# A state-space scan, attention and a mixture of experts on one core: two PSUM buffers for the first image's scan inputs, ranks by broadcasts, group norm sums on ScalarE

## The chip, the core and the metric

One core of a Trainium2 chip runs the whole program. The metric is the device time of one execution in microseconds (us). The engines' short names are those of the profile: PE (TensorE), DVE (VectorE), ACT (ScalarE), POOL (GpSimd), SP (SyncE, which issues nearly all DMAs here).

## What is computed

Four images of 384 channels by 32 x 32 positions go through two layers. Cut to what matters:

```python
# layer 0: group norm over 32 groups, then a selective scan in four directions
xs = _cross_scan(_gn(x))                      # rows, columns, both reversed: K = 4
x_dbl = einsum('bkdl,kcd->bkcl', xs, x_proj_weight)
dts, Bs, Cs = x_dbl[:, :, :12], x_dbl[:, :, 12:28], x_dbl[:, :, 28:]
dt = softplus(einsum('bkrl,kdr->bkdl', dts, dt_projs_weight) + dt_projs_bias)
# for each image, direction, channel d and state n (16 states), along 1024 positions:
h = h * exp(dt * A[d, n]) + (dt * u) * B[n]
y = sum over n of h * C[n]
y = _cross_merge(ys + Ds * u)
x = x + gelu(layernorm_over_channels(y))
# layer 1, on 1024 tokens of 384
t = t + causal_attention(_ln_t(t))            # one head of 384
z = _ln_t(t)
probs = softmax(z @ gate_w + gate_b)          # 4 experts
masked = probs of the two largest, others 0, divided by their sum + 1e-9
t = t + sum over e of masked[e] * (gelu(z @ w1[e] + b1[e]) @ w2[e] + b2[e])
```

Ties in the two largest go to the lower index. Everything is float32.

## The kernel before

**Units.** A scan instruction works on 128 partitions by 1024 positions: 32 channels by 4 states. An image has 192 such units (`IMAGE`: 3 chunks of 128 channels, 4 directions, 4 groups of states, 4 groups of 32 channels), four images have 768. For unit n, `decay` (L505) makes exp(dt*A) on ACT, `front` (L512) makes v = (dt*u) * B on DVE into PSUM (`ps_b`, one buffer of two banks), `middle` (L518) is the scan h on DVE, `back` (L525) multiplies h by C in place on POOL, and `row` (L550) sums over states on PE into another two banks, for four units at a time. The dt and dt*u of 32 channels, each repeated on four partitions, come by DMA from a scratch in DRAM (`spread_dt`, L473: tiles dt4 and du4, four buffers each); B and C come as one tile bc for four units by two DMAs (`spread_bc`, L484; two buffers). `fetch(t)` issues dt4 for unit t+5, du4 for t+3 and, where t+3 is a multiple of four, bc for t+3.

**Order.** The program is written out by hand. A loop over ticks t issues, in this order: `decay(t+2)`, what `due` holds for the tick, `front(t)`, `back(t-1)` with an added wait on `front(t)` ("beside a scan"), what `inner` holds, parked generators (`unpark`), `middle(t)`, `row(t-2)` on every fourth tick, `fetch(t)`, one step of the preparation of a later image, and then PE work. Each engine runs its own instructions in this order. PE work comes from generators that yield the time they expect to need; a tick grants 4.4 us of it in attention (`PACE_A`) and 3.3 in the experts (`PACE_E`). "wait" n puts a generator off by n ticks, "inner" parks it until the next tick's place between `back` and `middle`.

**Preparation.** `preparation(b)` does `groupnorm` (bn_stats L302, bn_aggr L303, then group means by small matmuls), `project_x` (rows of B and C, and the low-rank dt) and `project_dt` (softplus on ACT, the product dt*u on DVE, L395, and their stores to DRAM), for image b while the image before is scanned. `fold` (in `later`) multiplies the query and key weights in the first image.

**PE's banks.** Four PSUM banks (`banks`, class `Shared`) are taken and given back by name in first-in order; each taking makes a new tile. `project_dt` needs two at once.

**After an image's scans** `evict` (L570) and `finish` (layer norm, gelu, the sum with x, L707) leave the tokens yb. `behind(b)` then runs `attention(b)` and `experts(b)`, one image after the other. `attention` takes the buffer `a0` for its normalised tokens axn at its start; the same buffer holds `both` (named fx in the profile) of the experts of the image before, whose half `acc` is stored to `out` by `store` (L999), four ticks after the last expert. The subtraction of the mean into axn is L601, its last factor L649. `gates` finds each token's two best experts by comparing each expert with the others, one after the other (L901 to L915), with 16 elements in a partition.

The last image's attention and experts have nothing beside them: the scans end at 3237 us.

Of the kernel before, what the change touches and what calls it, by code (L numbers as in the profile page):

```python
# [15 lines left out]
P = 128  # L16
# [31 lines left out]
def hybrid_kernel(  # L48
# [53 lines left out]
    class Shared:  # L102
# [20 lines left out]
        def give(self, *names):  # L123
            for name in names:
                self.free.append((clock[0] + self.rest, self.taken.pop(name)))

    banks = Shared(
        BANKS, lambda i, name: ps_m.tile([P, 512], F32, tag=f"pm{i}", name=name), 0
    )
    slots = Shared(  # L130
        SLOTS, lambda i, name, *shape: slotp.tile(list(shape), F32, tag=f"s{i}", name=name), 1
# [68 lines left out]
    a4 = const.tile([P, K * NG, NQ], F32, tag="a4", name="a4")  # L200

    sel = const.tile([P, DJ], F32, tag="sel", name="sel")
    dump = const.tile([P, 1], F32, tag="dump", name="dump")
    nc.scalar.activation(a_raw, a_raw, AF.Exp)
    nc.scalar.activation(dump, eps, AF.Sqrt)
# [91 lines left out]
    def groupnorm(b, u):  # L297
        st = sm.tile([P, M, NH, 6], F32, tag="gn_st", name=f"gn_st_{b}")
        mv = sm.tile([P, M, 2], F32, tag="gn_mv", name=f"gn_mv_{b}")
        for m in range(M):  # L300
            for h in range(NH):
                nc.vector.bn_stats(st[:, m, h, :], u[m][:, h * 512 : (h + 1) * 512])  # L302
            nc.vector.bn_aggr(mv[:, m, :], st[:, m].rearrange("p h s -> p (h s)"))  # L303
            if b == 0 and m == 0:
                pgb = group_weights()
            yield "wait", 1
        if b == 0:
            nc.vector.tensor_scalar_mul(gback, pgb[:NGRP, :C], float(C // NGRP))
        mean_c = sm.tile([P, M], F32, tag="gn_mc", name=f"gn_mc_{b}")
        nc.vector.tensor_copy(mean_c, mv[:, :, 0])  # L310
        yield "wait", 1
        mean = sm.tile([P, M], F32, tag="gn_mean", name=f"gn_mean_{b}")
        ps = yield from over_group(mean_c, f"mean_{b}")
        nc.vector.tensor_copy(mean, ps)
        banks.give(f"gn_mean_{b}")
        dev = sm.tile([P, M], F32, tag="gn_dev", name=f"gn_dev_{b}")
        nc.vector.tensor_sub(dev, mean_c, mean)
        nc.vector.tensor_mul(dev, dev, dev)
        nc.vector.tensor_add(dev, dev, mv[:, :, 1])
        yield "wait", 1  # L320
        rstd = sm.tile([P, M], F32, tag="gn_rstd", name=f"gn_rstd_{b}")
        ps = yield from over_group(dev, f"var_{b}")
        nc.scalar.activation(rstd, ps, AF.Sqrt, bias=eps)
        banks.give(f"gn_var_{b}")
        yield "wait", 1
        nc.vector.reciprocal(rstd, rstd)
        nc.vector.scalar_tensor_tensor(mean, mean, -1.0, rstd, ALU.mult, ALU.mult)
        for m in range(M):
            if b == 0 and m == 1:
                nc.vector.tensor_scalar(  # L330
                    u[m], u[m], rstd[:, m : m + 1], mean[:, m : m + 1], ALU.mult, ALU.add
                )
            else:
                nc.scalar.activation(
                    u[m], u[m], AF.Identity, bias=mean[:, m : m + 1], scale=rstd[:, m : m + 1]
                )
            nc.sync.dma_start(xn_d[b][:, m, :], u[m])
            yield "wait", 1
# [169 lines left out]

    def front(n):
        u = units[n]  # L510
        u["v"] = ps_b.tile([P, L], F32, tag="v", name=f"v_{u['name']}")
        return nc.vector.tensor_tensor(u["v"], spread["du4", n], spread["bc", n][:, 0, :], ALU.mult)  # L512

    def middle(n):
# [62 lines left out]
            waiting.append(behind(b))  # L577


    def layernorm(dst, src, name, lag):  # L580

        width = dst.shape[2]
        n = width // 512
        mus = []
        for h in range(n):  # L590
            mu = yield from banks.take(f"mu_{name}_{h}")
            for c in range(M):
                nc.tensor.matmul(
                    mu, mean_w, src[:, c, bass.ts(h, 512)], start=(c == 0), stop=(c == M - 1)
                )
            mus.append(mu)
            yield "pe", 2.6
        yield "inner", 0
        for h in range(n):
            s = bass.ts(h, 512)  # L600
            nc.vector.tensor_tensor(  # L601
                dst[:, :, s], src[:, :, s], mus[h].unsqueeze(1).to_broadcast([P, M, 512]),
                ALU.subtract,
            )
            banks.give(f"mu_{name}_{h}")
        sqs = []
        for c in range(M):
            sq = yield from slots.take(f"sq_{name}_{c}", P, width)
            sqs.append(sq)
        for h in range(n):  # L610
            for c in range(M):
                s = bass.ts(h, 512)
                nc.scalar.activation(sqs[c][:, s], dst[:, c, s], AF.Square)
        yield "wait", lag
        var = yield from banks.take(f"var_{name}")
        for h in range(n):
            for c in range(M):
                for q in range(4):
                    o = h * 512 + q * P
                    nc.tensor.matmul(  # L620
                        var[32 * q : 32 * (q + 1), h * P : (h + 1) * P], mean_w[:, :32],
                        sqs[c][:, o : o + P], start=(c == 0), stop=(c == M - 1),
                        tile_position=(0, 32 * q),
                    )
            yield "pe", 1.0
        slots.give(*[f"sq_{name}_{c}" for c in range(M)])
        rs = one.tile([P, n, P], F32, tag=f"rs{n}", name=f"rs_{name}")
        nc.scalar.activation(
            rs, var[:, : n * P].rearrange("p (h t) -> p h t", t=P), AF.Sqrt, bias=eps
        )  # L630
        banks.give(f"var_{name}")
        yield "wait", 1
        nc.vector.reciprocal(rs, rs)
        yield "wait", lag
        backs = []
        for h in range(n):
            spread_ = yield from banks.take(f"rb_{name}_{h}")
            for q in range(4):
                nc.tensor.matmul(
                    spread_[:, q * P : (q + 1) * P],  # L640
                    ident[:, 32 * q : 32 * q + 1].to_broadcast([P, P]), rs[:, h, :],
                    start=True, stop=True,
                )
            backs.append(spread_)
            yield "pe", 1.0
        yield "inner", 0
        for h in range(n):
            s = bass.ts(h, 512)
            nc.vector.tensor_tensor(  # L649
                dst[:, :, s], dst[:, :, s], backs[h].unsqueeze(1).to_broadcast([P, M, 512]),  # L650
                ALU.mult,
            )
            banks.give(f"rb_{name}_{h}")

    def fold():

# [55 lines left out]
            defer(1 + m // 2, add)  # L712

    def attention(b, yb, fx0):
        xn = ap0.tile([P, M, L], F32, tag="a0", name=f"axn_{b}")
        gw_ = []
        for name, w in ((f"wg_{b}", g_d), (f"wv_{b}", wv.rearrange("(c p) d -> p c d", p=P))):
            ta = yield from slots.take(f"{name}a", P, 2, C)
# [1 line left out]
            tb = yield from slots.take(f"{name}b", P, C)  # L720
            nc.sync.dma_start(tb, w[:, 2, :])
            gw_.append((ta[:, 0, :], ta[:, 1, :], tb))
        yield from layernorm(xn, yb, f"at_{b}", 0)
        qt = htp.tile([P, M, L], F32, tag="ht", name=f"qt_{b}")
        vt = htp.tile([P, L // P, C], F32, tag="ht", name=f"vt_{b}")

# [141 lines left out]
    def gates(b, h, xn):  # L868
# [27 lines left out]
        nc.vector.tensor_reduce(red, sc, AX.X, ALU.add)  # L896
        nc.vector.reciprocal(red, red)
        nc.vector.tensor_tensor(sc, sc, over(red), ALU.mult)
        cnt = sm.tile([P, 4, E], F32, tag="cnt", name=f"cnt_{name}")
        cmp = sm.tile([P, 4, E], F32, tag="cmp", name=f"cmp_{name}")  # L900
        nc.vector.memset(cnt, 0.0)  # L901
        for d in range(E):

            other = sc[:, :, d : d + 1]
            if d > 0:
                nc.vector.tensor_tensor(
                    cmp[:, :, :d], other.to_broadcast([P, 4, d]), sc[:, :, :d], ALU.is_gt
                )
                nc.vector.tensor_add(cnt[:, :, :d], cnt[:, :, :d], cmp[:, :, :d])
            if d < E - 1:  # L910
                nc.vector.tensor_tensor(
                    cmp[:, :, d + 1 :], other.to_broadcast([P, 4, E - 1 - d]),
                    sc[:, :, d + 1 :], ALU.is_ge,
                )
                nc.vector.tensor_add(cnt[:, :, d + 1 :], cnt[:, :, d + 1 :], cmp[:, :, d + 1 :])  # L915
            if d % 2:
                yield "wait", 1
        mk = sm.tile([P, 4, E], F32, tag="mk", name=f"mk_{name}")
        nc.vector.scalar_tensor_tensor(mk, cnt, 1.5, sc, ALU.is_lt, ALU.mult)
        nc.vector.tensor_reduce(red, mk, AX.X, ALU.add)  # L920
# [32 lines left out]
    def experts(b, acc, xns):  # L953
# [43 lines left out]
        def store(h):  # L997
            o = h * 512
            nc.sync.dma_start(out[b, :, o : o + 512].rearrange("(m p) l -> p m l", p=P), acc)  # L999
            if h + 1 < NH:  # L1000
                defer(4, lambda: load(h + 1))

        load(0)
        for h, e in [(h, e) for h in range(NH) for e in range(E)]:
# [62 lines left out]
                    defer(2, out_, inner)  # L1067
            if e == E - 1:

                defer(4, lambda h=h: store(h))  # L1070

    pace = [PACE_E]

    def behind(b):
        while b not in finished:
# [78 lines left out]
    side.append(later())  # L1154
    decay(0)
    decay(1)
    t = 0
    while t < NU + 4 or waiting or side or due or inner or parked:
        clock[0] = t
# [2 lines left out]
        for f in due.pop(t, []):  # L1162
            f()
        done = None
        if t < NU:
            done = front(t)
        if 1 <= t <= NU:
            back(t - 1, done)
        for f in inner.pop(t, []):
# [67 lines left out]
```

## Time and profile before

| | us |
|---|---|
| median of 3 runs | 3911.18 (3906.58 to 3912.17) |
| the profiled execution | 3911.65 |
| its span, first to last instruction | 3909.9 |
| first tick's v (L512) starts | 49.3 |
| last scan of the first image ends | 789.0 |
| last scan of all ends | 3237.6 |

| engine | busy us | share of span |
|---|---|---|
| PE | 3382.8 | 87% |
| DVE | 3096.5 | 79% |
| ACT | 1887.9 | 48% |
| POOL | 1809.5 | 46% |

A line of the profile's groups names the source line, the engine, the operation, what is written and read, shapes and count, then busy us and mean ns of one, then the engine's idle time before these instructions and what ended it. In a timeline the two first numbers are start and length in us; idle time before the instruction stands in brackets. A chain of waits is followed back from the last instruction, at each step to what released it. DVE instructions overlap a little in the records where one doesn't depend on the one before.

### The profile page before, as it was taken

What the parts mean: (1) busy time and instruction counts of PE and PEld (TensorE: products, weight loads), DVE (VectorE), ACT (ScalarE), POOL (GpSimd) and SP (SyncE); (2) the same over time, 40 slices, a digit from 0 to 9 for tenths busy, and PEclk for the clock granted to TensorE, in tenths of its full rate; (3) what the DMA queues carried; (4) which work ended last, traced back from release to release, by engine and by line L of the source; (5) the groups of instructions that cost most, each with busy time, mean ns of one, the idle gap of its engine ahead of it and who ended that gap; (6) DMA issues with size and microseconds to landing.
All of it is one profiled execution on the core that took longest, in us unless ns stands there. A gap on an engine that the chain in (4) does not pass through costs nothing.

```text
span 3909.9 us, 32087 instructions
## 1 busy us (share of the span) xinstructions
PE 3382.8 (87%) x10623; PEld 1389.4 (36%) x10623; DVE 3096.5 (79%) x2258; ACT 1887.9 (48%) x1996; POOL 1809.5 (46%) x776
## 2 busy tenths in 40 slices
PE   4554655659899999978999999799999998999999
PEld 1100100015433334435433343354334334644444
DVE  6999999998999999979999899989999993110000
ACT  5442543446656656546656545555455453322121
POOL 2665666654555556535555566455566661000000
PEclk7665666679899999989999999899999999999999
DMA  5554545453576667535666666426566651132321
GB/s 192 203 183 148 197 147 188 162 189 127 191 239 208 236 223 241 184 112 190 223 211 214 212 218 213 162 105 227 179 214 213 222 187 44 61 90 82 96 82 55
DMA packets 406087, 671.85 MB, mean 172 GB/s; under 512 B 33265, under 2 KB 280353, under 8 KB 405921
## 3 DMA queue, kind: packets, MB, share of 16 engines
q1 hardware_dynamic: 399712, 669.41, 50.5%
q8 instruction: 84, 1.38, 0.1%
q10 hardware_dynamic: 6208, 0.39, 0.1%
q14 instruction: 83, 0.67, 0.1%
HBM read 597.75 MB, written 71.96 MB: 171 GB/s over the span
## 4 chain that ended last, share of the span: by engine, by line
DVE 49%; PE 38%; issue 5%; ACT 4%; DMA 2%; POOL 1%; DVEq 1%; SPq 0%; POOLq 0%; ACTq 0%
DVE h L518 29%; DVE v L512 15%; PE ph L1027 13%; PE fy L1052 12%; PE y L550 3%; PE ss L766 2%; PE pq L737 2%; PE pv L748 2%; PE po L832 1%; ACT da L505 1%; DVE fy L1061 1%; ACT ht L1016 1%; PE pxd L350 1%; DMA du<-dts 1%; DVE du L395 1%
## 5 line engine op out<-in xcount | busy, mean ns | idle before, releaser
L525 POOL TENSOR_TENSOR h<-h,bc 128x1024 f32<-128x1024 f32 x768 | 1808.4, 2355 | 1430.0 <-DVE v L512 1278.1
L518 DVE TENSOR_TENSOR_SCAN h<-da,v 128x1024 f32<-128x1024 f32 x768 | 1755.5, 2286 | 86.1 <-DVE v L512 1.5
L505 ACT ACTIVATE da<-dt,a 128x1024 f32<-128x1024 f32 x768 | 878.0, 1147 | 1232.3 <-DVE h L518 1171.7
L1027 PE MATMUL ph<-fx,w 128*128 128x512 f32 x2304 | 1027.5, 602 | 9.4 <-ACT ht L1012 3.8
L1052 PE MATMUL fy<-ht,w 128*128 128x512 f32 x2304 | 1015.8, 598 | 2.4 <-ACT dt L387 0.9
L512 DVE TENSOR_TENSOR v<-du,bc 128x1024 f32<-128x1024 f32 x768 | 947.2, 1233 | 38.5 <-DMA du<-dts 16.4
L550 PE MATMUL y<-h,sel 128*32 128x512 f32 x3072 | 703.7, 713 | 309.5 <-POOL h L525 295.3
L1027 PEld LDWEIGHTS ph<-fx,w 128*128 128x128 f32 x2304 | 434.8, 192 | 588.9 <-issue 530.7
L1052 PEld LDWEIGHTS fy<-ht,w 128*128 128x128 f32 x2304 | 435.5, 191 | 570.5 <-issue 551.7
L1012 ACT ACTIVATE ht<-ph,b1s 128x512 f32<-128x512 f32 x384 | 257.6, 679 | 453.0 <-PE ph L1027 452.5
L550 PEld LDWEIGHTS y<-h,sel 128*32 128x32 f32 x3072 | 118.3, 118 | 831.7 <-POOL h L525 579.2
L1061 DVE SCALAR_TENSOR_TENSOR fy<-fy,b2s,tw 128x512 f32<-128x512 f32 x96 | 72.3, 754 | 424.1 <-PE fy L1052 424.1
L1016 ACT ACTIVATE ht<-ht 128x3072 f32<-128x3072 f32 x64 | 176.9, 2764 | 0.8
L505 ACT ACT_TABLE_LOAD x110 | 141.1, 1283 | 14.4 <-DMA dt<-dts 12.5
L766 PE MATMUL ss<-axn,qt 128*128 128x512 f32 (+3 forms) x288 | 105.3, 512 | 7.4 <-ACT yb L844 5.8
L832 PE MATMUL po<-pt,vt 128*128 128x256 f32 x480 | 103.6, 363 | 6.7 <-ACT pt L728 6.7
L832 PEld LDWEIGHTS po<-pt,vt 128*128 128x128 f32 x480 | 91.9, 193 | 21.7 <-ACT pt L728 9.2
L780 DVE TENSOR_REDUCE nb<-ss 128x1 f32<-128x512 f32 (+3 forms) x48 | 26.2, 554 | 82.8 <-PE ss L771 64.6
L381 PE MATMUL pdt<-xd,wdt 12*128 12x512 f32 x184 | 61.5, 690 | 34.4 <-ACT xd L354 26.5
L766 PEld LDWEIGHTS ss<-axn,qt 128*128 128x128 f32 x288 | 52.3, 199 | 53.3 <-issue 36.5
L1064 DVE TENSOR_TENSOR fx<-fx,fy 128x512 f32<-128x512 f32 x96 | 65.9, 687 | 3.3
L1016 ACT ACT_TABLE_LOAD x50 | 64.2, 1283 | 0.9
(183 smaller groups left out, 1406.5 us busy)
## 6 DMA issues: line engine op xcount, KB each, us to landing
bc<-rows SPq DMA_DIRECT2D x384, 512.0 KB, 4.7
w<-in_w SPq DMA_DIRECT2D x384, 384.0 KB, 6.0
dt<-dts SPq DMA_DIRECT2D x192, 512.0 KB, 4.0
du<-dts SPq DMA_DIRECT2D x192, 512.0 KB, 6.1
dts<-dt SPq DMA_DIRECT2D x48, 512.0 KB, 4.9
dts<-du SPq DMA_DIRECT2D x48, 512.0 KB, 4.6
fx<-t2d SPq DMA_DIRECT2D x12, 768.0 KB, 6.0
tw<-mkd SPq DMA_DIRECT2D x32, 256.0 KB, 5.7
```

What stands on the lines that cost most here:

```text
L505: nc.scalar.activation(u["da"], spread["dt4", n], AF.Exp, scale=a4[:, g, u["q"] : u["q"] + 1])
L512: return nc.vector.tensor_tensor(u["v"], spread["du4", n], spread["bc", n][:, 0, :], ALU.mult)
L518: nc.vector.tensor_tensor_scan(u["h"][:, ::step], u["da"][:, ::step], u["v"][:, ::step], 0.0, op0=ALU.mult, op1=ALU.add,)
L525: product = nc.gpsimd.tensor_tensor(h, h, spread["bc", n][:, 1, :], ALU.mult)
L550: nc.tensor.matmul(y, sel, h, start=first, stop=last, tile_position=(0, jj * DJ))
L766: nc.tensor.matmul(ps[:, : e - o], qt[:, c, i * P : (i + 1) * P], xn[:, c, o:e], start=(c == 0), stop=(c == M - 1 and e <= i * P),)
L832: nc.tensor.matmul(pv[:, o:], vt[:, j, m * P : (m + 1) * P], pts[step][j // 4][:, j % 4, o:], start=False, stop=(j == nj - 1),)
L1012: nc.scalar.activation(ht[:, f, :], ps, AF.Identity, bias=bias)
L1016: nc.scalar.activation(ht, ht, AF.Gelu)
L1027: nc.tensor.matmul(ps, tiles[n][:, c, (f % 2) * P : (f % 2 + 1) * P], xns[h][:, c, :], start=(c == 0), stop=(c == M - 1),)
L1052: nc.tensor.matmul(pss[m], tiles[n][:, f, :], hts[fh][:, f, :], start=(fh == 0 and f == 0), stop=(fh == 1 and f == FH - 1),)
L1061: nc.vector.scalar_tensor_tensor(ps, ps, b2s[:, e, m : m + 1], tw, ALU.add, ALU.mult)
```

## The change

- **Scan inputs.** The last two of the four banks become slices of one tile `wide` of two banks. In the first image odd units have v there, even units in the old buffer. `front(0)` is issued ahead of the loop; then tick t issues `front(t+1)` before `middle(t)`, so the product for the next unit stands ahead of this unit's scan, and `back(t-1)` waits for `front(t+1)`. Meanwhile PE has two banks; it gets the other two back at tick 192, from which on the order is as before.
- **Group norm sums.** For images 1 to 3 the mean and the variance of a channel are made on ACT: Identity with scale -1/L and a sum into `mean_c`, then Square with that as bias and a sum, six activations on 128 x 1024, one a tick. Image 0 keeps bn_stats.
- **axn.** `attention` takes the buffer only after the two matmul groups of the mean have been issued and the store of the image before has been issued (`stored`). The store is put off by three ticks in place of four.
- **Ranks.** Two comparisons of all pairs by broadcasts (128 x 4 x 4 x 4), a product with a constant lower triangle, a maximum and a sum.

```diff
+    wide = ps_m.tile([P, 2, 512], F32, tag="wide", name="wide")
     banks = Shared(
-        BANKS, lambda i, name: ps_m.tile([P, 512], F32, tag=f"pm{i}", name=name), 0
+        BANKS,
+        lambda i, name: wide[:, i - BANKS + 2, :] if i >= BANKS - 2
+        else ps_m.tile([P, 512], F32, tag=f"pm{i}", name=name),
+        0,
     )
...
+    lower = const.tile([P, E, E], F32, tag="lower", name="lower")
+    nc.vector.memset(lower, 0.0)
+    for e in range(1, E):
+        nc.vector.memset(lower[:, e, :e], 1.0)
...
     def groupnorm(b, u):
...
+        mean_c = sm.tile([P, M], F32, tag="gn_mc", name=f"gn_mc_{b}")
+        if b > 0:
+            var_c = sm.tile([P, M], F32, tag="gn_vc", name=f"gn_vc_{b}")
+            sq = yield from slots.take(f"gn_sq_{b}", P, L)
+            for m in range(M):
+                nc.scalar.activation(
+                    sq, u[m], AF.Identity, scale=-1.0 / L, accum_out=mean_c[:, m : m + 1]
+                )
+                yield "wait", 1
+            for m in range(M):
+                nc.scalar.activation(
+                    sq, u[m], AF.Square, bias=mean_c[:, m : m + 1], accum_out=var_c[:, m : m + 1]
+                )
+                yield "wait", 1
+            slots.give(f"gn_sq_{b}")
+            nc.vector.tensor_scalar_mul(mean_c, mean_c, -1.0)
+            nc.vector.tensor_scalar_mul(var_c, var_c, 1.0 / L)
-        for m in range(M):
+        for m in range(M) if b == 0 else ():
...
     def front(n):
         u = units[n]
-        u["v"] = ps_b.tile([P, L], F32, tag="v", name=f"v_{u['name']}")
+        if n < IMAGE and n % 2:
+            u["v"] = wide.rearrange("p b t -> p (b t)")
+        else:
+            u["v"] = ps_b.tile([P, L], F32, tag="v", name=f"v_{u['name']}")
...
     def layernorm(dst, src, name, lag, b=0, into=None):
...
             yield "pe", 2.6
+        if into is not None:
+            while b > 0 and b - 1 not in stored:
+                yield "wait", 1
+            dst = into()
         yield "inner", 0
...
     def attention(b, yb, fx0):
-        xn = ap0.tile([P, M, L], F32, tag="a0", name=f"axn_{b}")
...
-        yield from layernorm(xn, yb, f"at_{b}", 0)
+        xn = yield from layernorm(
+            None, yb, f"at_{b}", 0, b,
+            lambda: ap0.tile([P, M, L], F32, tag="a0", name=f"axn_{b}"),
+        )
...
+        cmp = [one.tile([P, 4, E, E], F32, tag=f"cmp{i}", name=f"cmp{i}_{name}") for i in range(2)]
+        each = sc.unsqueeze(3).to_broadcast([P, 4, E, E])
+        other = sc.unsqueeze(2).to_broadcast([P, 4, E, E])
+        nc.vector.tensor_tensor(cmp[0], other, each, ALU.is_gt)
+        nc.vector.tensor_tensor(cmp[1], other, each, ALU.is_ge)
+        nc.vector.tensor_tensor(
+            cmp[1], cmp[1], lower.unsqueeze(1).to_broadcast([P, 4, E, E]), ALU.mult
+        )
+        nc.vector.tensor_tensor(cmp[0], cmp[0], cmp[1], ALU.max)
         cnt = sm.tile([P, 4, E], F32, tag="cnt", name=f"cnt_{name}")
...
+        nc.vector.tensor_reduce(cnt, cmp[0], AX.X, ALU.add)
+        yield "wait", 1
...
             if h + 1 < NH:
                 defer(4, lambda: load(h + 1))
+            else:
+                stored.add(b)
...
-                defer(4, lambda h=h: store(h))
+                defer(3, lambda h=h: store(h))
...
+    held_back = [entry for entry in banks.free if entry[1] >= BANKS - 2]
+    for entry in held_back:
+        banks.free.remove(entry)
+    front(0)
...
-        if t < NU:
+        if t + 1 < IMAGE:
+            done = front(t + 1)
+        elif IMAGE <= t < NU:
             done = front(t)
+        if t == IMAGE:
+            banks.free.extend(held_back)
```

More of the change, by code (lines that the diff above doesn't have):

```diff
@@ L308, in groupnorm @@
             nc.vector.tensor_scalar_mul(gback, pgb[:NGRP, :C], float(C // NGRP))
-        mean_c = sm.tile([P, M], F32, tag="gn_mc", name=f"gn_mc_{b}")
-        nc.vector.tensor_copy(mean_c, mv[:, :, 0])
+            var_c = mv[:, :, 1]
+            nc.vector.tensor_copy(mean_c, mv[:, :, 0])
         yield "wait", 1
@@ L318, in groupnorm @@
         nc.vector.tensor_mul(dev, dev, dev)
-        nc.vector.tensor_add(dev, dev, mv[:, :, 1])
+        nc.vector.tensor_add(dev, dev, var_c)
         yield "wait", 1
@@ L577, in evict, with layernorm @@
             waiting.append(behind(b))
-    def layernorm(dst, src, name, lag):
-        width = dst.shape[2]
+    def layernorm(dst, src, name, lag, b=0, into=None):
+        width = src.shape[2]
         n = width // 512
@@ L653, in layernorm @@
             banks.give(f"rb_{name}_{h}")
+        return dst
     def fold():
@@ L898, in gates @@
         nc.vector.tensor_tensor(sc, sc, over(red), ALU.mult)
-        cnt = sm.tile([P, 4, E], F32, tag="cnt", name=f"cnt_{name}")
[L900 to L917, printed above, removed]
+        cmp = [one.tile([P, 4, E, E], F32, tag=f"cmp{i}", name=f"cmp{i}_{name}") for i in range(2)]
[7 more added lines that the diff above has]
+        nc.vector.tensor_tensor(cmp[0], cmp[0], cmp[1], ALU.max)
+        cnt = sm.tile([P, 4, E], F32, tag="cnt", name=f"cnt_{name}")
+        nc.vector.tensor_reduce(cnt, cmp[0], AX.X, ALU.add)
+        yield "wait", 1
         mk = sm.tile([P, 4, E], F32, tag="mk", name=f"mk_{name}")
@@ L1068, in experts @@
             if e == E - 1:
-                defer(4, lambda h=h: store(h))
+                defer(3, lambda h=h: store(h))
     pace = [PACE_E]
+    stored = set()
     def behind(b):
@@ L1156, in hybrid_kernel @@
     decay(1)
+    assert len(banks.free) == BANKS
+    held_back = [entry for entry in banks.free if entry[1] >= BANKS - 2]
+    for entry in held_back:
+        banks.free.remove(entry)
+    front(0)
     t = 0
```

## The prediction

> **What bounds the kernel now.** I read the page's chain of work first, then its groups, then the busy time by stage, then timelines of single stages. Chain (shares by engine, by line) and three groups of the page:
>
> ```profile
> DVE 49%; PE 38%; issue 5%; ACT 4%; DMA 2%; POOL 1%; DVEq 1%; SPq 0%; POOLq 0%; ACTq 0%
> ...
> L525 POOL TENSOR_TENSOR h<-h,bc 128x1024 f32<-128x1024 f32 x768 | 1808.4, 2355 | 1430.0 <-DVE v L512 1278.1
> L518 DVE TENSOR_TENSOR_SCAN h<-da,v 128x1024 f32<-128x1024 f32 x768 | 1755.5, 2286 | 86.1 <-DVE v L512 1.5
> ...
> L512 DVE TENSOR_TENSOR v<-du,bc 128x1024 f32<-128x1024 f32 x768 | 947.2, 1233 | 38.5 <-DMA du<-dts 16.4
> ```
>
> Each of 768 units takes one v (1.233 us) and one scan (2.287 us) on DVE, and one product of 2.35 us on POOL that waits for a v. The stages differ (first image, then the experts beside the third image's scans, then the tail without scans):
>
> ```profile
> 60.00:776.00 716.00, 412.63 (x918) 69.20 (x921) 684.75 (x415) 326.23 (x306) 437.67 (x187) 0.62 0.49 174
> 1860.00:2500.00 640.00, 620.68 (x1938) 250.33 (x1931) 600.51 (x422) 365.81 (x353) 363.01 (x155) 0.97 0.62 209
> 3237.00:3909.00 672.00, 655.65 (x1869) 316.02 (x1867) 86.70 (x151) 170.77 (x220) 3.02 (x2) 0.98 0.25 73
> ```
>
> (Columns: PE, PEld, DVE, ACT, POOL.) In the first image DVE is 96% busy and PE 58%: DVE alone sets the time. Later PE (97%) and DVE (94%) are both full, so a gain of one is kept only in part. The tail is PE's. A gain before the first image ends (789 us) moves all that follows.
>
> The first image's steady tick, from the timeline (start, length):
>
> ```profile
> 500.83 1.23 DVE L512 TENSOR_TENSOR v<-du,bc 128x1024 f32<-128x1024 f32 x1
> 502.19 2.29 DVE L518 TENSOR_TENSOR_SCAN h<-da,v 128x1024 f32<-128x1024 f32 x1
> 502.29 2.35 POOL L525 TENSOR_TENSOR h<-h,bc 128x1024 f32<-128x1024 f32 x1 [1.40 <-DVE v L512]
> 504.51 1.23 DVE L512 TENSOR_TENSOR v<-du,bc 128x1024 f32<-128x1024 f32 x1
> ```
>
> A v every 3.688 us. Between v and its scan lie 0.133 us; scan to v 0.035. The product starts 0.170 us after v's end, 0.230 on every fourth tick (a new bc). Two more places matter:
>
> ```profile
> 1672.79 0.69 DVE L1064 TENSOR_TENSOR fx<-fx,fy 128x512 f32<-128x512 f32 x1
> 1673.39 2.28 DVE L518 TENSOR_TENSOR_SCAN h<-da,v 128x1024 f32<-128x1024 f32 x1
> ```
>
> A scan behind work it doesn't depend on starts 0.08 us before that work's recorded end. And a v that begins well inside a product is held:
>
> ```profile
> 812.15 1.51 DVE L512 TENSOR_TENSOR v<-du,bc 128x1024 f32<-128x1024 f32 x1
> ...
> 810.23 2.34 POOL L525 TENSOR_TENSOR h<-h,bc 128x1024 f32<-128x1024 f32 x1 [1.70 <-PE y L550]
> ```
>
> The product ends at 812.57; v ends 1.09 us later, at 813.66. All six v that overlap a product by 0.36 to 0.44 us end 1.09 us after it.
>
> **The Trainium skill.** "SBUF — State Buffer", Who interferes with whom: a DVE instruction with two SBUF inputs contends with a GpSimd instruction that reads SBUF, and the one that comes second waits for the whole of the other. The trace agrees (1.51 for 1.23 us above); the scan, with v in PSUM, runs beside the product at 2.287 us. "VectorE: DVE Perf Modes", The DRAIN you can't avoid: a following instruction starts when the pipe is empty, and a semaphore costs nothing extra. Here it does: 0.133 us behind its own v, -0.08 behind other work. "ScalarE: Activation LUTs", What ACT_TABLE_LOAD costs: 280 ns + 0.833 ns an element with a bias operand, so 1.13 us for 1024 as an estimate; the trace has 1.23 for the normalising activation (L334), and 0.195 for an accumulator read (L784). Neither Identity at L334 nor Square at L613 has a table load in the groups.
>
> **The change, part by part** (against the profiled execution: 3911.65 us, span 3909.9; the median of the runs, 3911.18, is the same within 0.5).
>
> 1. *v one unit ahead, first image.* The scan no longer follows its own v: 0.133 becomes about -0.085, and DVE alone could do a tick in 3.47. But POOL binds first: product end to v end 1.09, v end to the next product 0.17 (0.23 on each fourth), product 2.346 (median of this stage): 3.605 or 3.665, mean 3.62. So 0.068 a tick, not 0.22. 155 of the 192 ticks are clean 3.688 ones: -10.5. The 22 ticks with a du product (L395; two SBUF inputs, so held by POOL in the same way) come out at 4.75 either way.
>
> 2. *What now waits for transfers sooner.* DVE is in order: a v whose du or bc is late now also holds the scan of the unit before, which has its data. Start of the program:
>
> ```profile
> 48.34 9.09 DMA du<-dts
> ...
> 415.41 9.41 DMA du<-dts
> ```
>
> (chain, start and length). du of unit 2 lands at 57.4; before, two scans were done by then, afterwards one, as v of 1 and v of 2 precede the scans of 0 and 1. Unit 2's scan goes from 58.86 to 62.15: +3.3, of which the missing v ahead of the last scan gives back 1.2: +2.1.
>
> In the steady state bc's load is released by a product that ends with a scan, so it had three ticks, and now has two:
>
> ```profile
> 500.91 1.16 SPq L484 DMA_DIRECT2D bc<-rows  x2
> ...
> DMA to landing us min/median/max: 3.4/4.6/8.7
> ```
>
> This load is for the unit whose v began at 511.89; the v before it began at 508.20. From issue to the new need: 7.3 us less 0.1 for the shorter ticks. The second of the pair is issued 0.6 us later, so it needs 5.2 at the median, up to 9.3. A load of du has some 9 us from its issue and takes 3.4 to 10.0 (median of du and dt 5.9). Landings later than the start of the previous v, where the trace has them: bc of units 16, 32, 96, 160 by 1.0, 0.8, 4.0, 0.4; du of 33, 81, 97 by 3.4, 1.9, 4.1 (units 32 and 33, and 96 and 97, count once; 0.8 of the stall at 96 and 97 was there before): about 10 us. About half of the landings are not recorded, which would add; but the two largest come from SP standing behind the preparation's own transfers, which the change moves. I take +8, between +3 and +16.
>
> 3. *Two banks fewer in the first image.* project_dt needs two banks at once and must alternate with fold, one side waiting a few ticks. Its results are due 20 or more ticks later: 0.
>
> 4. *Group norm sums on ScalarE* (images 1 to 3). Off DVE: per chunk two bn_stats and an aggregation, 1.42 us net of overlaps:
>
> ```profile
> 860.09 1.26 DVE L302 BATCH_NORM_STATS2 gn_st<-x 128x6 f32<-128x512 f32 x2
> 861.39 0.21 DVE L303 BATCH_NORM_AGGREGATE gn_mv<-gn_st 128x2 f32<-128x12 f32 x1
> ```
>
> Image 1's stand in three ticks of 4.97, which become 3.62: -4.0. Image 2's lie on the chain to the first attention (860 to 876): -4.3, less 0.8 for ACT and two small multiplications: -3.5. Image 3's (1435 to 1450) lie where PE is full: between 0 and -4.3, taken -2. On ACT six activations of 1.13 to 1.23 plus 0.2 each, one a tick; ACT is 46% busy in the first image and runs its exp two ticks ahead of the scan: 0 where that cover holds, at most 1.4 a tick if it failed. Three ticks later than before: not due.
>
> 5. *Ranks.* Thirteen small instructions (about 2.1 us a call: rows L901 to L915) become five on 64 elements, some 0.23 each (estimate from 0.175 for 16 elements): 1.3. Saves 0.9 in each of eight calls; two are in the tail, the others beside attention: 0 to -5.4, taken -2.
>
> 6. *axn allocated after the store, store one tick earlier.* Before, DVE stood at the subtraction until the store had read the buffer:
>
> ```profile
> 1696.04 3.42 DVE L601 TENSOR_TENSOR axn<-yb,mu_at 128x1536 f32<-128x1536 f32 x2 [9.38 <-DMA out<-fx]
> ...
> 2523.35 3.42 DVE L601 TENSOR_TENSOR axn<-yb,mu_at 128x1536 f32<-128x1536 f32 x2 [2.42 <-DMA out<-fx]
> ```
>
> Behind it stood v, scans and products. Afterwards the subtraction comes two ticks later in DVE's order for image 1, one for image 2. The store at 1689.07 stood behind a bc load in SP's queue; one tick earlier it goes before it, at 1686.7, and lands near 1693.5, when DVE, not stopped, arrives: PE's attention starts 2.3 earlier; for image 2, 1.1 later. DVE is three ticks further than PE, so three ticks' worth of expert work (3.3 each) moves behind the last scan, where it can fill the 5.7 us that PE is idle there. Between -7 and +4: -3.
>
> Sum: -10.5 + 2.1 + 8 - 4.0 - 3.5 - 2 - 2 - 3 = -14.9; 3911.65 - 14.9 = 3897. All terms at their ends together give 3882 to 3916; most of that lies in 3885 to 3909.
>
> **Rivals.**
> A. The product doesn't hold v after all: ticks of 3.47, another -0.15 x 155 = -23, of which +6 in later landings: 3880. Against it: the six held v, all at 1.09. 8%.
> B. Transfers bind, slower. Mechanism: in-order DVE at v, price one for one from 7.2 us after issue. All my gains without the +8 are 22.9, so it decides from there: 0.5 us of lateness on each of 47 groups. With 0.75 each (loads 1.5 us longer than the medians, as where preparation and fold transfer too) 35 in place of 8: 3924. For it: maxima of 8.7 and 10.0; against: most lie 1 to 4 us inside. 13%.
> C. Given back: only parts 1, 2 and image 1's sums count (-4.4), since PE is full later: 3907. 17%.
> D. Part 6 costs: three ticks at attention's pace (4.4) lost to PE, +13 for -3: 3913. 5%.
>
> The forecast has 57%. About 0.2% (8 us) is what can be told from no change. Faster: 0.48 of the forecast, A, 0.05 of C: 0.61. Slower: B, 0.02 of C, 0.03 of D: 0.18. Same: 0.21. The range takes in A, C and D and leaves B out: 3878 to 3916; the forecast's own is 3885 to 3909.
>
> **What would show it.** Ticks of 3.61 and 3.67 with v longer than 1.233 (held by POOL) in the first image, scans 0.08 before v's end; ticks of 3.47 mean A. v preceded by idle ended by bc or du, some 5 to 16 us before the last scan of image 0: above 23, B. No bn_stats after 20 us. No idle at L601 by out<-fx in images 1 and 2. The first attention some 8 us earlier, the last scan more than that. I am wrong if image 0's last scan comes no earlier than before, or if the gain there is gone by the tail.

## The result, and the profile after

| | before | changed kernel |
|---|---|---|
| median, us | 3911.68 (3906.58 to 3913.57, 4 runs) | 4102.17 (4098.15 to 4104.17, 4 runs) |
| ratio | | 1.0488, 95% interval 1.0470 to 1.0506 |
| span of the profiled execution | 3909.9 | 4100.8 |
| last scan of the first image starts | 786.8 | 781.6 |
| last scan of all starts | 3235.3 | 3402.0 |
| PE busy, us | 3382.8 | 3437.9 |

The change costs 190 us where 15 us of gain had been forecast. The third and fourth rows of times already say where to look: the first image, in which the new order runs, ended 5.1 us *earlier* (4.4 had been forecast for it). Images 1 to 3, whose order of units is the old one, lost 172 us, and the tail without scans, in which PE finishes what is left, another 24 (span less the last scan's start: 674.6 before, 698.8 after).

The page of the changed kernel: its chain by engine and by line, then groups (the scan and v have two forms now, one for each buffer).

```profile
PE 44%; DVE 14%; ACT 6%; issue 2%; DMA 1%; DVEq 0%; POOL 0%; SPq 0%; ACTq 0%; POOLq 0%
PE wide L1086 10%; PE wide L1061 8%; PE fy L1086 8%; PE ph L1061 8%; DVE h L548 8%; DVE v L542 4%; PE y L580 3%; ACT ht L1050 1%; ACT ht L1046 1%; ACT da L532 1%; PE wide L775 1%; PE ss L804 1%; PE wide L804 1%; PE wide L786 1%; PE wide L870 1%
...
L555 POOL TENSOR_TENSOR h<-h,bc 128x1024 f32<-128x1024 f32 x768 | 1807.3, 2353 | 1597.7 <-DVE v L542 1331.2
L548 DVE TENSOR_TENSOR_SCAN h<-da,v 128x1024 f32<-128x1024 f32 x672 | 1534.6, 2284 | 95.3 <-PE y L580 33.9
...
L542 DVE TENSOR_TENSOR v<-du,bc 128x1024 f32<-128x1024 f32 x672 | 840.8, 1251 | 40.6 <-DMA du<-dts 19.2
L1061 PE MATMUL wide<-fx,w 128*128 128x512 f32 x1122 | 555.0, 635 | 109.0 <-ACT ht L1046 82.7
...
L1061 PE MATMUL ph<-fx,w 128*128 128x512 f32 x1182 | 544.4, 604 | 6.5 <-DMA w<-in_w 3.7
```

The scan and the product on POOL take as long as before (2.284 and 2.353 us); what changed is who sets the end: DVE had 49% of the chain, now 14%. And `wide`, meant for the scan's input in the first image, stands in PE's expert lines. L1061 is the first product of an expert. Of its 2304 matmuls 1182 go into a bank of their own (`ph`), with 6.5 us of idle before them; 1122 go into a slice of `wide`, with 109.0 us of idle, most of it ended by ACT's read (L1046). Before, all 2304 were one group:

```profile
L1027 PE MATMUL ph<-fx,w 128*128 128x512 f32 x2304 | 1027.5, 602 | 9.4 <-ACT ht L1012 3.8
```

Three stages of the changed kernel (first image; experts beside the third image's scans; tail; columns PE, PEld, DVE, ACT, POOL busy, the granted clock, the DMA share, GB/s):

```profile
60.00:776.00 716.00, 410.48 (x914) 73.75 (x915) 697.73 (x410) 326.95 (x313) 440.11 (x188) 0.62 0.49 175
1940.00:2612.00 672.00, 620.03 (x1903) 246.52 (x1902) 594.65 (x402) 361.26 (x348) 360.45 (x153) 0.96 0.58 197
3404.00:4100.00 696.00, 664.53 (x1881) 316.49 (x1879) 84.94 (x135) 170.11 (x220) 2.71 (x2) 0.99 0.24 71
```

In the middle stage PE went from 97% to 92% and DVE from 94% to 88%: neither is full any more. The waits view of the whole run names what they wait for (us in total, times, longest; PEld is PE's loading of weights, and its waits are in part the same time as PE's own):

```profile
PEld wide L1061 <- ACT ht L1046: 126.5, 55, 7.8
PE wide L1061 <- ACT ht L1046: 82.7, 46, 7.0
DVE wide L1095 <- ACT ht L1046: 56.4, 9, 14.7
```

L1095 works on an expert's second product and L1046 reads a first product, so the two are in different slices. Before, DVE had no such wait, PE's own for this read was 3.8 us (the group line above), and the weight loads had

```profile
PEld ph L1027 <- ACT ht L1012: 25.4, 33, 4.6
```

The tail shows such waits by themselves. Timeline (start, length, idle before in brackets):

```profile
3717.59 5.31 PE L1061 MATMUL wide<-fx,w 128*128 128x512 f32 x12
3722.74 2.74 PE L1061 MATMUL ph<-fx,w 128*128 128x512 f32 x6
3722.94 1.26 ACT L1046 ACTIVATE ht<-wide,b1s 128x512 f32<-128x512 f32 x2 [4.46 <-PE wide L1061]
3725.32 2.74 PE L1061 MATMUL wide<-fx,w 128*128 128x512 f32 x6
3728.09 0.69 ACT L1046 ACTIVATE ht<-wide,b1s 128x512 f32<-128x512 f32 x1 [1.89 <-PE wide L1061]
3728.83 2.84 PE L1061 MATMUL wide<-fx,w 128*128 128x512 f32 x6 [0.78 <-ACT ht L1046]
```

Six matmuls fill a bank in some 2.6 us. Banks are given out in the order in which they came back, so the twelve at 3717.59 are both slices, one after the other. ACT, idle since 3718.5, could have read the first at about 3720.3 (an estimate: the start and the 2.74 us of six); it reads both from 3722.94, when the second is done. So a read of one slice waits for the matmuls last issued into the other. The last line is the reverse: matmuls into one slice wait until ACT's read of the other, from 3728.09 to 3728.78, is over. In the kernel before the same stage is one row of matmuls with a read after each group of six:

```profile
3600.13 0.69 ACT L1012 ACTIVATE ht<-ph,b1s 128x512 f32<-128x512 f32 x1 [1.89 <-PE ph L1027]
3602.70 0.69 ACT L1012 ACTIVATE ht<-ph,b1s 128x512 f32<-128x512 f32 x1 [1.89 <-PE ph L1027]
```

PE's idle time rose from 527.1 to 662.9 us (span less busy), +136, and its busy time by 55 with the same 10,623 matmuls; together these are the 191 us of span. The first product's matmuls alone are busy 72 us longer (555.0 + 544.4 against 1027.5), and most of that is in the slices' group (635 ns a matmul, against 604 in the banks of their own). Part of a wait is thus recorded as work: of the six matmuls at 3728.83 the first, which had waited, has 697 ns, the others 592.

### The profile page after: what moved, and what is told of

Its sections match the earlier page's. It is cut to its first block, busy times and chain, and to the rows that moved or that the text cites. A ratio compares the mean times of both kernels' runs of the same rounds, so it can differ in the third digit from the quotient of the medians.

```text
span 4100.8 us, 31774 instructions
## 1 busy us (share of the span) xinstructions
PE 3437.9 (84%) x10623; PEld 1407.6 (34%) x10623; DVE 3093.9 (75%) x2174; ACT 1902.9 (46%) x2028; POOL 1808.4 (44%) x776
## 3 DMA queue, kind: packets, MB, share of 16 engines
q8 instruction: 84, 1.38, 0.1%
## 4 chain that ended last, share of the span: by engine, by line
PE 44%; DVE 14%; ACT 6%; issue 2%; DMA 1%; DVEq 0%; POOL 0%; SPq 0%; ACTq 0%; POOLq 0%
PE wide L1086 10%; PE wide L1061 8%; PE fy L1086 8%; PE ph L1061 8%; DVE h L548 8%; DVE v L542 4%; PE y L580 3%; ACT ht L1050 1%; ACT ht L1046 1%; ACT da L532 1%; PE wide L775 1%; PE ss L804 1%; PE wide L804 1%; PE wide L786 1%; PE wide L870 1%
## 5 line engine op out<-in xcount | busy, mean ns | idle before, releaser
L548 DVE TENSOR_TENSOR_SCAN h<-da,v 128x1024 f32<-128x1024 f32 x672 | 1534.6, 2284 | 95.3 <-PE y L580 33.9
L1061 PE MATMUL wide<-fx,w 128*128 128x512 f32 x1122 | 555.0, 635 | 109.0 <-ACT ht L1046 82.7
L1086 PE MATMUL wide<-ht,w 128*128 128x512 f32 x1272 | 565.9, 598 | 14.5 <-DVE fx L1098 8.5
L1061 PE MATMUL ph<-fx,w 128*128 128x512 f32 x1182 | 544.4, 604 | 6.5 <-DMA w<-in_w 3.7
L1086 PE MATMUL fy<-ht,w 128*128 128x512 f32 x1032 | 462.5, 600 | 0.0
L1095 DVE SCALAR_TENSOR_TENSOR wide<-wide,b2s,tw 128x512 f32<-128x512 f32 x53 | 40.0, 754 | 441.5 <-PE wide L1086 385.0
L1061 PEld LDWEIGHTS wide<-fx,w 128*128 128x128 f32 x1122 | 217.4, 201 | 424.1 <-issue 250.1
L1086 PEld LDWEIGHTS wide<-ht,w 128*128 128x128 f32 x1272 | 239.5, 191 | 331.5 <-issue 296.8
L1061 PEld LDWEIGHTS ph<-fx,w 128*128 128x128 f32 x1182 | 225.9, 194 | 310.4 <-issue 288.8
L1046 ACT ACTIVATE ht<-ph,b1s 128x512 f32<-128x512 f32 x197 | 133.8, 681 | 406.7 <-PE ph L1061 406.5
L1086 PEld LDWEIGHTS fy<-ht,w 128*128 128x128 f32 x1032 | 195.4, 192 | 255.1 <-issue 248.7
L1046 ACT ACTIVATE ht<-wide,b1s 128x512 f32<-128x512 f32 x187 | 126.6, 683 | 257.4 <-PE wide L1061 251.4
L548 DVE TENSOR_TENSOR_SCAN h<-da,wide 128x1024 f32<-128x1024 f32 x96 | 218.3, 2274 | 0.0
```

Source lines behind the costliest of these rows:

```text
L548: nc.vector.tensor_tensor_scan(u["h"][:, ::step], u["da"][:, ::step], u["v"][:, ::step], 0.0, op0=ALU.mult, op1=ALU.add,)
L1046: nc.scalar.activation(ht[:, f, :], ps, AF.Identity, bias=bias)
L1061: nc.tensor.matmul(ps, tiles[n][:, c, (f % 2) * P : (f % 2 + 1) * P], xns[h][:, c, :], start=(c == 0), stop=(c == M - 1),)
L1086: nc.tensor.matmul(pss[m], tiles[n][:, f, :], hts[fh][:, f, :], start=(fh == 0 and f == 0), stop=(fh == 1 and f == FH - 1),)
```

## The experiments

**One part alone: the shared tile in the kernel before.** Nothing but where PE's last two banks lie is changed; no unit of the scan uses them.

```diff
+    wide = ps_m.tile([P, 2, 512], F32, tag="wide", name="wide")
     banks = Shared(BANKS, lambda i, name:
-        ps_m.tile([P, 512], F32, tag=f"pm{i}", name=name), 0)
+        wide[:, i - BANKS + 2, :] if i >= BANKS - 2
+        else ps_m.tile([P, 512], F32, tag=f"pm{i}", name=name), 0)
```

> The kernel before with one edit: PE's last two banks are slices of one tile of two banks; order, group norm, ranks and store as before. Theory W (instructions on one slice wait for those on the other, since the waits are kept for the whole tile): 4060 to 4120 us, most of the loss in images 1 to 3 and some 15 us in the tail; ph and fy matmuls named wide wait for ACT and DVE. Rival O (the loss comes from the new order of work: sums on ScalarE, the later axn, v one unit ahead): 3905 to 3920.

4076.84 us (4064.14 to 4079.45), ratio 1.0418 (1.0403 to 1.0432). The tile alone costs 166 of the 190 us: 134 up to the last scan, and 32 in the tail, where some 15 had been expected. Its first image is unchanged (unit 191 starts 0.2 earlier than before); PE is 58% busy there.

**The rest without it.** The changed kernel with own banks and v just ahead of its scan; the sums on ScalarE, the ranks and the later axn stay.

```diff
-        if n < IMAGE and n % 2:
-            u["v"] = wide.rearrange("p b t -> p (b t)")
-        else:
-            u["v"] = ps_b.tile([P, L], F32, tag="v", ...)
+        u["v"] = ps_b.tile([P, L], F32, tag="v", ...)
...
-        if t + 1 < IMAGE:
-            done = front(t + 1)
-        elif IMAGE <= t < NU:
+        if t < NU:
             done = front(t)
```

> The changed kernel without its first part: four own banks, v in one buffer and just ahead of its scan, as before; sums on ScalarE, ranks by broadcasts and the later axn stay. Theory W: 3890 to 3905 (the terms of the prediction for these parts sum to -14.5). Rival O: above 4000.

3905.39 us (3900.74 to 3913.19), ratio 0.9987 (0.9981 to 0.9994): -5.4, just past the slow end of what had been expected.

**All parts, the tile given up at tick 192.** The two-bank tile lies in a pool of its own (a stretch of memory from which the program cuts tiles), which is closed at tick 192; PE then gets two tiles of one bank from a pool opened in its stead.

```diff
+    ps_w = tc.tile_pool(name="ps_w", bufs=1, space=PSUM)
+    late = [ps_w.__enter__()]
-    wide = ps_m.tile([P, 2, 512], F32, tag="wide", name="wide")
+    wide = late[0].tile([P, 2, 512], F32, tag="wide", name="wide")
...
         if t == IMAGE:
+            ps_w.__exit__(None, None, None)
+            late.insert(0, ctx.enter_context(tc.tile_pool(name="ps_n", bufs=1, space=PSUM)))
             banks.free.extend(held_back)
```

> The changed kernel with all its parts, but the tile of two banks lives only until tick 192; from then on PE's last two banks are tiles of their own, a new one at each taking, as before. Theory W: 3880 to 3905, as the prediction had it; the first image as in the changed kernel (last scan 5 us earlier than before). Rival O: above 4000.

3904.86 us (3902.23 to 3908.97), ratio 0.9985 (0.9978 to 0.9992). The loss is gone with everything else in place. So it is neither v ahead, nor the two banks PE lacks in the first image, but the slices of one tile after tick 192. It also prices "v one unit ahead": 0.5 us against the run above, which can't be told from nothing.

**One slice, or one own bank.** Is a slice slow in itself, or only beside the other? Both kernels leave PE three banks after tick 192: the changed kernel with one slice given back, and the last one with one own bank given back.

```diff
-            banks.free.extend(held_back)
+            banks.free.extend(held_back[:1])
```

> The changed kernel, but at tick 192 PE gets back only one of the two slices, so that it works with three banks, one of them a slice of the shared tile. Theory W (a slice waits for the work on the other slice): with the other slice unused after the first image nothing is left to wait for, so the same as the next kernel (three own banks) within 0.5%. Rival S (a slice of a tile that lives long is slow by itself, for instance since no new tile is made at each taking): about as much slower than the next kernel as half of the loss, 60 us or more.

> Three own banks from tick 192 on, the two-bank tile given up there. Against the swapped kernel with four own banks (3905) a bank fewer costs PE work some time: 3910 to 4000 under both theories; it is the yardstick for the kernel with one slice.

3950.41 us, 1.0105 (1.0092 to 1.0119), and 3948.02 us, 1.0100 (1.0085 to 1.0115): the same. A slice whose neighbour isn't used costs what a bank of its own costs. Three banks, of whatever kind, cost about 40 us; that is less than four of which two are tied together. The loss has another shape, too: with three banks the scans end sooner than with four own ones (the last starts at 3214.9 and 3211.8, against 3231.3), but 2010 of PE's matmuls come after that, against 1878, so PE's work was put off into the tail.

**The order in which the banks are taken.** From tick 192 a taking prefers own banks and slices in turn, or two and two; free banks only.

```diff
+                want = self.count % 2        # paired: self.count // 2 % 2
+                at = next((j for j, e in enumerate(self.free)
+                           if (e[1] >= BANKS - 2) == bool(want)), 0)
+                self.count += 1
-            i = self.free.pop(0)[1]
+            i = self.free.pop(at)[1]
```

> From tick 192 on a taking prefers, in turn, an own bank and a slice of the shared tile (oldest free one of that kind, else the oldest of all), so that two slices seldom stand one behind the other on PE. If the cost comes from slices that follow each other, most of the 190 us go: 3920 to 3990. If it comes from any use of a slice, whatever stands between: within 20 us of the changed kernel, 4080 to 4120.

> The same rule with two own banks in turn and then two slices, so that the slices stand one behind the other as often as can be. If following slices are the cause: not faster than the changed kernel, 4095 to 4180. If the order of the banks does not matter: the same as the run with alternation, whatever that is.

4034.42 us, 1.0324 (1.0307 to 1.0341), and 4116.22 us, 1.0534 (1.0519 to 1.0550). The order alone moves the time by 82 us, and the waits go with it. With alternation (waits view, as above):

```profile
PEld wide L1069 <- ACT ht L1054: 45.7, 34, 5.8
...
DVE wide L1103 <- ACT ht L1054: 42.6, 9, 14.7
...
PE wide L1069 <- ACT ht L1054: 16.5, 13, 2.5
```

and in pairs:

```profile
PEld wide L1069 <- ACT ht L1054: 120.1, 57, 8.6
PE wide L1069 <- ACT ht L1054: 73.5, 48, 7.7
```

But alternation was expected at 3920 to 3990, or at 4080 and above, and it lies between: it takes 68 us off and keeps 125 of loss. In its trace no two groups of the first product go into slices one directly behind the other, matmuls of the scans' sums left out (in pairs, 77 times; in the changed kernel, 58). So direct succession there is well under half of the loss. DVE's wait at the second product (L1103) is mostly left, 42.6 of 56.4 us, in nine places in either run. The rest can lie in that product, whose sums `fy` are held over two groups of matmuls while other banks turn round; that wasn't tried.

**The sums in three ticks.** Why did the rest, without the tile, bring -5.4 and not the -14.5 that parts 4 to 6 have in the sum? In that run's trace DVE stands twice in the preparation of image 2:

```profile
1228.87 2.29 DVE L541 TENSOR_TENSOR_SCAN h<-da,v 128x1024 f32<-128x1024 f32 x1
1238.16 1.22 DVE L418 TENSOR_TENSOR du<-dt,ut 128x1024 f32<-128x1024 f32 x1 [7.00 <-ACT dt L410]
...
1247.85 1.23 DVE L418 TENSOR_TENSOR du<-dt,ut 128x1024 f32<-128x1024 f32 x1 [4.90 <-PE fy L1079]
```

The first product dt*u waits for dt on ACT; on ACT, dt stands behind a read of `ph`, and that waits for a block of expert matmuls:

```profile
1230.52 4.88 PE L1054 MATMUL ph<-fx,w 128*128 128x512 f32 x6
...
1235.44 0.69 ACT L1039 ACTIVATE ht<-ph,b1s 128x512 f32<-128x512 f32 x1 [1.94 <-PE ph L1054]
```

The second product's wait ends with expert matmuls as well (L1079). Before, the same two products stood two ticks earlier in the order and met no such block: the ticks at units 288 and 289 took 4.73 and 5.18 us, here those at 290 and 291 take 11.79 and 9.69. The sums take six ticks, one activation each; this run puts the two activations of a chunk into one tick (other parts as in the run without the tile).

```diff
                     sq, u[m], AF.Identity, scale=-1.0 / L, accum_out=mean_c[:, m : m + 1]
                 )
-                yield "wait", 1
-            for m in range(M):
                 nc.scalar.activation(
```

> The kernel without the shared tile (own banks, v just ahead of its scan; 3905), with the two activations of a chunk in one tick, so that the sums take three ticks as bn_stats did and the preparation keeps its old places. Theory T (the 12 us that DVE stood at two du products near tick 290 come from the preparation lying three ticks later): no such stall, du at ticks 288 and 289, 3890 to 3898. Rival L (they come from the load of the sums on ACT): still about 3905.

3892.57 us (3891.91 to 3894.46), ratio 0.9961 (0.9948 to 0.9973), -16.1. The stall is gone:

```profile
1214.11 1.22 DVE L416 TENSOR_TENSOR du<-dt,ut 128x1024 f32<-128x1024 f32 x1
1219.17 1.22 DVE L416 TENSOR_TENSOR du<-dt,ut 128x1024 f32<-128x1024 f32 x1 [0.31 <-PE ph L1052]
```

and PE's attention of image 1 starts at 1693.9 instead of 1708.3. ACT still does the same six activations, so the stall came from the place of the preparation and not from their load. But the stall is not all that the place cost: unit 288, ahead of it, already starts 9.7 us earlier than in the run with six ticks (1211.8 against 1221.5), unit 300 then 21.3, and the tail gives some back (681.1 against 671.5). Where those 9.7 us come from wasn't looked into.

**The store and axn undone** (axn taken at the attention's start, the store after four ticks; otherwise the run without the tile).

```diff
-            while b > 0 and b - 1 not in stored:
-                yield "wait", 1
...
-                defer(3, lambda h=h: store(h))
+                defer(4, lambda h=h: store(h))
```

> The kernel without the shared tile (3905), with axn taken at attention's start and the store after four ticks, as in the kernel before: the third part undone. If that part gains what the prediction said (3 us, ends -4 to 7): 3901 to 3912, likeliest 3908; DVE again stands 9 and 2 us at the subtraction for the store.

3907.15 us (3905.81 to 3911.73), ratio 0.9999 (0.9991 to 1.0007), beside 3905.39 with the part. The part is worth 2 us by the medians, 5 by the ratios; the intervals overlap, so it is not clear of nothing. The idle time that the part was to remove is small here anyway, against what had been expected:

```profile
1694.75 3.42 DVE L626 TENSOR_TENSOR axn<-yb,mu_at 128x1536 f32<-128x1536 f32 x2 [0.83 <-DMA out<-fx]
```

That is 0.83 us where before had 9.38 (in image 2, 2.98 where it had 2.42). Before this point DVE had stood at the two dt*u products, as in the run that this one is made from, so it came late. What the part is worth with the sums in three ticks, where DVE isn't late, wasn't tried.

**The whole change, repaired.** The pool closed at tick 192 and the sums in three ticks; beside it the three-tick run once more, on the same chip.

> All parts of the change, the two-bank tile given up at tick 192, and the sums on ScalarE in three ticks. If v one unit ahead is worth what the prediction's first two parts sum to (-0.4 us), the same as the kernel with own banks and three ticks (3892.6) within 4 us; if the shorter ticks count more than the transfers that are now late, 3880 to 3886; if less, 3898 and more.

> The kernel with own banks, v just ahead of its scan and the sums in three ticks once more, beside the last one on the same chip: 3892 to 3893 as before.

3892.35 us (3891.70 to 3895.28), 0.9955 (0.9942 to 0.9967), and 3893.72 us (3892.70 to 3895.13), 0.9957 (0.9943 to 0.9970). Both are faster than both kernels of the change, and they don't differ: with the rest in place, v one unit ahead brings nothing that can be seen. The last stages of the three-tick run, at its first trial (same columns as above):

```profile
1846.00:2486.00 640.00, 626.26 (x1972) 256.23 (x1972) 599.68 (x405) 366.96 (x355) 362.74 (x154) 0.97 0.63 214
3219.00:3890.00 671.00, 659.33 (x1882) 318.49 (x1874) 84.86 (x134) 171.16 (x221) 0.00 (x0) 0.99 0.25 74
```

PE is back at 98% in both.

## Why the prediction was wrong

The step that failed is part 3, "Two banks fewer in the first image", put at 0. It asked what PE lacks while the tile is the scan's, and there 0 was right as far as it shows: the first image's last scan starts at 781.2 with the tile given up at tick 192, and at 780.6 with four own banks throughout. It didn't ask what PE gets back at tick 192: two slices of one tile, and the traces show PE, ACT and DVE waiting between them as for one thing. No term of the sum and no rival has the images after the first paying for it. Measured: 166 us for the tile alone, and 197 between the changed kernel and the one with the pool closed. It stood in the diff's first lines, beside a PE that is 97% busy in the expert stage which the prediction itself shows.

**Part 1, v ahead.** As worked out. The first image's timeline of the changed kernel:

```profile
505.03 1.45 DVE L542 TENSOR_TENSOR wide<-du,bc 128x1024 f32<-128x1024 f32 x1
506.39 2.27 DVE L548 TENSOR_TENSOR_SCAN h<-da,v 128x1024 f32<-128x1024 f32 x1
506.65 2.34 POOL L555 TENSOR_TENSOR h<-h,bc 128x1024 f32<-128x1024 f32 x1 [1.26 <-DVE wide L542]
508.70 1.38 DVE L542 TENSOR_TENSOR v<-du,bc 128x1024 f32<-128x1024 f32 x1
510.00 2.27 DVE L548 TENSOR_TENSOR_SCAN h<-da,wide 128x1024 f32<-128x1024 f32 x1
512.30 1.38 DVE L542 TENSOR_TENSOR wide<-du,bc 128x1024 f32<-128x1024 f32 x1
```

From v to v 3.67 and 3.60 us (forecast 3.665 and 3.605), each v 1.38 to 1.45 in place of 1.233. The product of 506.65 ends at 508.99, the v beside it at 510.08, 1.09 later. All 158 v of the first image that start inside a product end 1.09 to 1.16 us after it. So the product does hold v, as the Trainium skill has it in "SBUF — State Buffer", Who interferes with whom; rival A is out.

**Part 2, late transfers.** Right in kind, and inside the range (+8, between +3 and +16). Between 60 and 800 us the v waited for du and bc in seven places, 12.7 us in all, against 0.5 before. One of them, and ahead of these the start of the program:

```profile
52.51 1.23 DVE L542 TENSOR_TENSOR wide<-du,bc 128x1024 f32<-128x1024 f32 x1 [2.79 <-DMA du<-dts]
...
362.35 1.23 DVE L542 TENSOR_TENSOR wide<-du,bc 128x1024 f32<-128x1024 f32 x1 [3.35 <-DMA du<-dts]
```

At the start unit 2 begins 3.4 us later than before (forecast +3.3). Against part 1's -10.5 the two forecast terms (+2.1 and +8) leave -0.4; the pairs of runs with and without v ahead differ by -0.5 and -1.4 us in the median. The first image's last scan says the same: 781.2 with v ahead and 780.6 without, 783.2 and 782.9 with three ticks. So the 5.1 us by which the changed kernel's first image ended earlier belong to the sums (part 4), and nothing of them can be put down to v. Rival B did not come: it needed 35 us.

**Part 4, the sums.** Image 1's gain was right: its preparation moved unit 88 by -4.7 against unit 80 (forecast -4.0, run without the tile). The activations took what was estimated from the skill and the trace: "ScalarE: Activation LUTs", What ACT_TABLE_LOAD costs, gives 280 ns + 0.833 ns an element for a bias in memory, an estimate of 1133 ns for 1024; the tile view of the changed kernel (ns: least, middle, most) has

```profile
L315 ACT ACTIVATE gn_sq<-x x9: 1040/1046/1062, 360.1 to 1535.1; 128x1024 f32<-128x1024 f32 x9
L320 ACT ACTIVATE gn_sq<-x,gn_mc x9: 1132/1135/1152, 374.1 to 1547.1; 128x1024 f32<-128x1024 f32 x9
```

But "Three ticks later than before: not due" is the second wrong term, by about 11 us (-16.1 against -5.4): the results were not due, yet everything behind them in the preparation moved too, and in image 2's it met expert work on PE. Three ticks of activations keep the old place.

**Parts 5 and 6.** The ranks were not tried alone; in the changed kernel's trace their five instructions take 1.11 us a call, where before thirteen took 2.11 (forecast 1.3 and 2.1). The store and axn are worth 2 to 5 us, with DVE late, in place of 3. With the tile's waits and the sums' delay taken out, the whole change brings -18.1 (3892.35 against 3910.44), beside the -14.9 of the sum. That these lie so near does not show each term: only v ahead, the store and the sums' places were priced by runs.

**The first attention** starts 7.8 us earlier in the changed kernel (872.5 against 880.3; forecast some 8). The condition under which the prediction called itself wrong, "if the gain there is gone by the tail", is what the trace shows: unit 224 still starts 3.8 us earlier than before, unit 272 already 25.5 later.

Open: the changed kernel loses 25 us more than the kernel before with the tile alone. The order of the banks can do that (it moved 82), but that it is this wasn't tried.

## What to carry over

When a buffer is lent out, price what the borrower's form does to the owner after it comes back, for as long as the owner uses it, not only while it's away. A slice of a larger tile is not a buffer of its own: if its waits are kept for the tile, a full engine that turns its buffers round pays for it (here 166 us for the tile alone), and separate tiles once the lending is over (here, a pool closed and another opened) cost nothing that could be seen. And a step that gets longer by ticks moves everything behind it in a hand-written order: look at what it will stand behind there, not only at when its result is due.

## What was not expected of the hardware

Nothing in the engines: scans and POOL's products took the same time in both kernels (2.284 and 2.286 us, 2.353 and 2.355), and v was held in the first image as forecast. The cost is one of the program's waits, for with the pool closed at tick 192 as many banks serve the same work without it. In reading a trace, though, part of it does not look like waiting: 55 of the 191 us are recorded as busy time of PE.
